# Five moves in a hand-written schedule: inputs, constants, values, slots and weight rows of a two-layer attention kernel

## The chip, the cores and the metric

The kernel runs on one core of a Trainium2 chip. The metric is the device time of one launch in microseconds (us). Three runs of the kernel before gave 1906.97, 1907.01 and 1912.09 us; the median is 1907.01.

## The reference

Sixteen batches of 256 tokens with 256 features (`x`) and a context of the same shape (`ctx`) pass through two layers, all in float32:

```python
x = x + xattn0(ctx, ln(x))     # 8 heads of 128; keys and values over [LN(ctx); LN(ln(x))], 512 rows
x = x + ffn0(ln(x))            # 1024 hidden, gelu; every batch has its own additions to W1 and W2:
                               #   products of rows 1..16 of ln(x), times a scale
x = x + xattn1(ln(x), ctx, ctx)   # one head of 256, softmax over 256 context rows
x = x + ffn1(ln(x))            # 8 experts of 256; sigmoid routing by zones, top 2 when no zone holds
```

The routing weights decide which expert serves which token. A token that an expert does not serve has weight zero there.

## The kernel before, in words

**Tiling.** A batch is two tiles of 128 tokens (TC = 2). Everything that must have features on the partitions is transposed in three steps: 32x32 blocks on VectorE (`to_blocks`, line 291), a write to DRAM (`hop`, line 296) and a read back in four DMAs (`from_blocks`, line 302). The probabilities of a head go the same way (`s2`, lines 863 and 867, and `s2_fetch`, line 876); the tile `tb` that holds their blocks has one buffer.

**The main loop** runs over 128 heads, n = 8b + h. One pass does: scores of head n (`s1`: sc, then maxima nm on VectorE, then exponentials on ScalarE), scaling by 1/sum on POOL (`s1_scale`), the fetch of head n-1's probabilities (`s2_fetch`), queries (`s0q`) and keys (`s0k`) of head n+1, the "bulk" of the head, the output product po of head n-2 (`s3`), and the transposes and hop of head n (`s2`). Evictions go through `evict`: to ScalarE, or to VectorE for a while after a gelu was emitted.

**Bulk.** In heads 2 to 5 a quarter of the values of heads 4-7 (pv), in heads 6 and 7 those of the next batch's heads 0-3, and in heads 0 to 4 one of the five steps of `inputs(b + 1)`: statistics of the context and its hop; statistics of x, normalised context and its hop; normalised x and its hop; and two steps of scaling on ScalarE into kvT.

**Chains and gaps.** What follows the eight heads of a batch is a generator `chain(b)`: output projection (px), layer norm (yb), the batch's own weights (W1e, W2e), hidden layer (ph), gelu, second product (pf), layer norm (yc), second attention (pv of WvT, pq of M1, scores, po), layer norm (row), routing logits (pl); then `route(b)`: weights, slot numbers (pn) and 16 indirect DMAs on POOL that write each token's row to its place in `slots_d`. Chains start at head 2 of the next batch and last nearly two batches, so that two chains and a route are open at once.

The planner keeps a count of TensorE time, `Clock.pe`, which each matmul raises. At each of six places of a head, `gap` runs units of the open jobs, oldest first, until 0.8 us of TensorE work were added. A unit ends with `yield w`: the job is not ready until `Clock.pe` has gone on by w. `SENT` (6.5) and `LANDED` (7.5) are the waits put behind a hop and behind its fetch. All of this fixes the program's order while it is built; on the chip each engine, and SP for the DMAs, takes its instructions in that order, and waits where data is missing.

**After the heads**, the same planner mixes the last chain with the experts (`experts`, class `G`): rows of one expert's slots are loaded (line 1082), transposed by a hop, multiplied (pg, pu, pd) and added to the output by indirect DMAs on POOL (line 1165). Groups of the second part of the batches (10 to 15) are loaded only after the route of batch 15 is done.

**The rows of the batch's own weights.** `chain` writes 8 rows of the layer norm to `ev_d` (lines 375 and 376) and reads them back to all 128 partitions as `ev` (line 380, 1 MB on the SBUF side). W1e (line 405, VectorE) and W2e (line 412, POOL; line 420, VectorE) are made of them and of `od` (line 397), which is taken from the transposed yb.

**The constants of the queries** are a product of yc with a row g1, summed (line 488): rc, used at the maxima of the second attention (lines 523 to 525).

Of the kernel before, what the change touches and what calls it, by code (L numbers as in the profile page):

```python
# [16 lines left out]
ALU = mybir.AluOpType  # L17
AX = mybir.AxisListType

P = 128  # L20
# [9 lines left out]
def xattn_ffn_kernel(  # L30
# [10 lines left out]
    nc = tc.nc  # L41
    B, S, D = x.shape
# [7 lines left out]
    TC = S // P  # L50
# [13 lines left out]
    wk = ctx.enter_context(tc.tile_pool(name="work_c", bufs=1))  # L64
# [49 lines left out]
    def gap(least=0.8, stand=0.0):  # L114
# [31 lines left out]
        out=before, in_=before, compare_op=ALU.is_gt, fill=0.0,  # L146
# [87 lines left out]
    g1 = keep.tile([P, D], F32, name="g1")  # L234
# [50 lines left out]
    def to_blocks(pool, src, C, tag, bufs, name, most=None):  # L285
        tb = pool.tile(
            [P, C * D], F32, tag=tag, bufs=bufs, name=name, padded_shape=[P, most or C * D]
        )
        tb = tb.rearrange("p (m d c s) -> p m d c s", m=QP, d=DC, c=C)
        for c in range(C):  # L290
            nc.vector.transpose(  # L291
                tb.rearrange("p m d c s -> p d m c s")[:, :, :, c, :],
                src[:, c, 0:D].rearrange("p (d m r) -> p d m r", d=DC, m=QP),
            )
        hop = dram.tile([P, QP, DC * C * QB], F32, tag=f"{tag}{C}", name=f"hop_{name}")
        nc.sync.dma_start(hop, tb.rearrange("p m d c s -> p m (d c s)"))
        return hop

    def from_blocks(dst, hop):
        from_ = hop.rearrange("(a r) m f -> m r a f", r=QB)  # L300
        for m in range(QP):
            nc.sync.dma_start(dst[ts(m, QB)].rearrange("r a d c s -> r a (d c s)"), from_[m])  # L302
# [22 lines left out]
    NA = D // NI  # L325


    behind_exp = []

    lasting = {}  # L330

    def chain(b, A, behind):
# [11 lines left out]
        def raw_tile(tag, name):  # L344
            return wk.tile([P, QP, DC, TC, QB], F32, tag=tag, name=name)
# [22 lines left out]
        while behind is not None and b - 1 not in A.fed:  # L368
# [2 lines left out]
        ln_apply(y, x_b, mv, rs)  # L371
        yp = wk.tile([32, NI, NA], F32, tag="yp", name=f"yp_{b}")
        nc.vector.tensor_copy(yp, y[0:32, 0, :].rearrange("p (a c) -> p c a", c=NI))
        ev_d = dram.tile([2 * NI, D], F32, tag="ev_d", name=f"ev_d_{b}")
        nc.sync.dma_start(ev_d[0:NI, :], y[1 : 2 * NI : 2, 0, :])
        nc.sync.dma_start(
            ev_d[NI : 2 * NI, :], yp[1 + 2 * NI : 4 * NI : 2, :, :].rearrange("p c a -> p (c a)")
        )
        ev = wk.tile([P, 2 * NI, D], F32, tag="ev", name=f"ev_{b}")
        nc.sync.dma_start(  # L380
            ev.rearrange("p n d -> p (n d)"),
            ev_d.rearrange("n d -> (n d)").partition_broadcast(P),
        )
        landed = Clock.pe + 15.0
        plus_row(x_b, lasting["b2"])
        hop = to_blocks(wk, y, TC, "tbc", 1, f"yb_{b}_b")
        yield SENT
        yTb = raw_tile("yT", f"ybT_{b}")
        from_blocks(yTb, hop)
        yT = in_order(yTb)  # L390
        yield landed - Clock.pe
        while behind is not None and b - 1 not in A.fed_forward:
            yield 0.4

# [89 lines left out]
        hop = to_blocks(wk, y, TC, "tbc", 1, f"yc_{b}_b")  # L484
        pr = wk.tile([P, TC, S], F32, tag="pr1", name=f"pr1_{b}")
        rc = small.tile([P, TC], F32, tag="rc", bufs=2, name=f"rc_{b}")
        for c in range(TC):
            nc.vector.tensor_tensor_reduce(
                out=pr[:, c, :], in0=y[:, c, :], in1=g1, op0=ALU.mult, op1=ALU.add,
                scale=1.0, scalar=g0, accum_out=rc[:, c : c + 1],  # L490
            )
        yield SENT
        yTc = raw_tile("raw_c", f"ycT_{b}")
        from_blocks(yTc, hop)
        landed = Clock.pe + LANDED


        v1 = wk.tile([P, TC, D], F32, tag="v1", name=f"v1_{b}")
        for m in range(TC):
            pv = mm_tile(D, f"pv1_{b}_{m}")  # L500
            for d in range(DC):
                mm(pv, cT[:, d, ts(m, P)], WvT[:, d, :], start=(d == 0), stop=(d == DC - 1))
            evict(v1[:, m, :], pv, None, None)
            yield
        yield landed - Clock.pe
        q1T = wk.tile([P, DC, S], F32, tag="q1T", name=f"q1T_{b}")
        for m in range(DC):
# [27 lines left out]
        pT = wk.tile([P, TC, S], F32, tag="pT1", bufs=1, name=f"pT1_{b}")  # L535
        for m in range(TC):
            evict(pT[:, m, :], in_order(raw)[:, m], None, None)
        yield 2.5
        mv = mv_tile("d")
        for c in range(TC):  # L540
            ri = small.tile([P, 1], F32, tag="ri1", name=f"ri1_{b}_{c}")
# [9 lines left out]

        rs = ln_rstd(mv, "d")
        nc.sync.dma_start(out[b].rearrange("(c p) d -> p c d", p=P), x_b)
        yield 2.8
        while b >= 2 and not A.tails[b - 2].done:
            yield 0.4
        row = A.row[b] = wk.tile([P, TC, ROW], F32, tag="row", bufs=2, name=f"row_{b}")
# [26 lines left out]
    def route(b, A, mine):  # L584
# [65 lines left out]
        serves, rest = tmp("serves"), tmp("rest")  # L650
        nc.vector.tensor_scalar(flat(serves), flat(wt), 0.0, None, ALU.is_gt)
        nc.vector.tensor_scalar(flat(rest), flat(wt), 0.0, None, ALU.is_le)
        yield 4.0

        pn = mm_tile(2 * TC * E, f"pn_{b}")
        mm(pn[:, 0 : TC * E], below, flat(serves), start=True, stop=True)
# [37 lines left out]
    with ExitStack() as sh, ExitStack() as sa, ExitStack() as sf:  # L694
# [315 lines left out]
        def bulk(b, h):  # L1010
            if h == 0:
                if b == 0:
                    filling["turns"] = all_turns()
                filling["in"] = inputs(b + 1) if b + 1 < B else None
            if h == 2:
                filling["v1"] = values(b, 1)
            if h == 6:
                filling["v0"] = values(b + 1, 0) if b + 1 < B else None
            if b == 0:
                load_late(h)  # L1020
                for _ in range(2):
                    advance(filling["turns"])
            if 2 <= h <= 5:
                advance(filling["v1"])
            if h <= 4:
                advance(filling["in"])
            if h == 7 and b + 2 < B:
                load_in(b + 2)
            if h >= 6:
                advance(filling["v0"])  # L1030
                yield
                advance(filling["v0"])
            yield
# [205 lines left out]
        for n in range(NS + 2):  # L1239
            b, h = divmod(n, H)  # L1240
            if h == 2 and b > 0:
                last = add_chain(b - 1, last)
            more = bulk(b, h) if n < NS else None
            if n < NS:
                s1(n)
            if n == NS - 4:
                sf.close()
                open_front()
                rest = Job(experts(
                    lists,  # L1250
                    lambda g: g.part == 0 or B - 1 in A.tails and A.tails[B - 1].done,
                ))
                line.append(rest)
            if n == NS - 1:
                sa.close()
                open_last_layer()
            while behind_exp:
                behind_exp.pop()()
            stand = 2.0 if n >= NS - 1 else 0.0
            gap(stand=stand)  # L1260
            if n < NS:
                s1_scale(n)
            if 1 <= n <= NS:
                s2_fetch(n - 1)
            if n + 1 < NS:
                s0q(n + 1)
            gap(stand=stand)
            if n + 1 < NS:
                s0k(n + 1)
            gap(stand=stand)  # L1270
            advance(more)
            gap(stand=stand)
            advance(more)
            gap(stand=stand)
            if n >= 2:
                s3(n - 2)
            gap(stand=stand)
            if n < NS:
                s2(n)
# [1 line left out]
        last = add_chain(B - 1, last)  # L1281
        line.append(rest)
        while line:
            while behind_exp:
                behind_exp.pop()()
            if D_.more is None and B - 1 in A.projected:
                sh.close()
                open_rest()
            gap(stand=1e9)
# [49 lines left out]
```

## Time and profile before

| what | value |
|---|---|
| median of three runs | 1907.01 us |
| profiled execution, its own time | 1906.59 us |
| its span | 1904.8 us |
| TensorE busy | 1824.0 us (96%) |
| VectorE busy | 1226.8 us (64%) |
| ScalarE busy | 593.1 us (31%) |
| POOL busy | 871.1 us (46%) |
| mean granted clock of TensorE | 0.989 |

The span runs from the first to the last instruction of the profiled execution. A row of the waits says: engine, what waited, its line, "<-", what ended the wait, and then us in total, times, longest. A row of the timeline says: start and duration in us, engine, line, operation, tile written <- tiles read, shapes, number of instructions merged, and in brackets the idle time before it with what ended it. Matmuls all stand on line 80 and are told apart by their tiles. A row of stretches gives the bounds, the length, busy time of PE, PEld, DVE, ACT and POOL with their counts, then the granted clock, the share of the DMA engines and GB/s. Heads of a batch begin with "sc<-kT,qT"; in batch 9, head 0 begins at 833.5, head 1 at 843.3, head 2 at 852.3, head 3 at 869.4, head 4 at 880.6, head 5 at 888.3 and head 6 at 898.8 us.

### The profile page before, as it was taken

What the parts mean: (1) busy time and instruction counts of PE and PEld (TensorE: products, weight loads), DVE (VectorE), ACT (ScalarE), POOL (GpSimd) and SP (SyncE); (2) the same over time, 40 slices, a digit from 0 to 9 for tenths busy, and PEclk for the clock granted to TensorE, in tenths of its full rate; (3) what the DMA queues carried; (4) which work ended last, traced back from release to release, by engine and by line L of the source; (5) the groups of instructions that cost most, each with busy time, mean ns of one, the idle gap of its engine ahead of it and who ended that gap; (6) DMA issues with size and microseconds to landing.
All of it is one profiled execution on the core that took longest, in us unless ns stands there. A gap on an engine that the chain in (4) does not pass through costs nothing. (4 is left out here: it accounts for less than half of the span.)

```text
span 1904.8 us, 22785 instructions
## 1 busy us (share of the span) xinstructions
PE 1824.0 (96%) x6568; PEld 1228.8 (65%) x6568; DVE 1226.8 (64%) x3324; ACT 593.1 (31%) x1323; POOL 871.1 (46%) x996
## 2 busy tenths in 40 slices
PE   8999999999999999999999999999999999899996
PEld 4666666666666666666666666666666767566665
DVE  4466586757575757585857575858574767565654
ACT  3433334333333333333333333333333212111110
POOL 2132226343535353535353535353534275767666
PEclk9999999999999999999999999999999999999999
DMA  6553536464636463636363636363636587999996
GB/s 214 177 188 122 167 133 216 140 200 136 200 131 204 133 213 130 199 126 212 128 216 128 212 127 203 126 214 126 219 118 202 157 224 194 232 246 234 216 206 109
DMA packets 274638, 336.92 MB, mean 177 GB/s; under 512 B 31772, under 2 KB 227272, under 8 KB 272456
## 3 DMA queue, kind: packets, MB, share of 16 engines
q1 hardware_dynamic: 243736, 283.82, 47.1%
q0 software_dynamic: 30720, 51.54, 11.4%
q8 instruction: 55, 0.90, 0.2%
q14 instruction: 79, 0.65, 0.1%
q10 hardware_dynamic: 48, 0.01, 0.0%
HBM read 167.87 MB, written 167.38 MB: 176 GB/s over the span
## 5 line engine op out<-in xcount | busy, mean ns | idle before, releaser
L855 POOL TENSOR_SCALAR pr<-pr,ri 128x512 f32<-128x512 f32 x256 | 182.5, 725 | 664.0 <-DVE ri L854 662.0
L847 ACT ACTIVATE pr<-sc,nm 128x512 f32<-128x512 f32 x256 | 173.5, 682 | 578.1 <-DVE nm L841 575.4
L674 POOL DMA_INDIRECT slots_d<-row,at_slot x256 | 255.6, 998 | 68.2 <-issue 68.2
L80 PE MATMUL sc<-kT,qT 128*128 128x512 f32 x512 | 253.1, 618 | 33.2 <-ACT kT L780 33.2
L80 PE MATMUL po<-pT,v 128*128 128x256 f32 x1024 | 243.3, 380 | 4.0 <-DMA pT<-hop 3.6
L1165 POOL DMA_INDIRECT out_dram<-o,at x128 | 200.0, 1563 | 99.2 <-DVE o L1164 27.1
L80 PE MATMUL pk<-kvT,Wk_sb 128*128 128x512 f32 x512 | 240.6, 592 | 0.0
L80 PE MATMUL pv<-Wv_sb,kvT 128*128 128x512 f32 x512 | 239.1, 596 | 0.1
L80 PEld LDWEIGHTS po<-pT,v 128*128 128x128 f32 x1024 | 194.4, 190 | 67.0 <-issue 37.7
L863 DVE STREAM_TRANSPOSE tb<-pr 128x512 f32<-128x512 f32 x256 | 165.6, 684 | 34.9 <-DMA hop<-tb 34.9
L80 PEld LDWEIGHTS sc<-kT,qT 128*128 128x128 f32 x512 | 98.0, 197 | 108.7 <-issue 64.8
L841 DVE TENSOR_REDUCE nm<-sc 128x1 f32<-128x512 f32 x256 | 160.3, 662 | 4.8 <-PE sc L80 3.8
L893 DVE TENSOR_SCALAR outT<-po,cvec 128x256 f32<-128x256 f32 x128 | 60.0, 469 | 157.8 <-PE po L80 137.6
L80 PEld LDWEIGHTS pv<-Wv_sb,kvT 128*128 128x128 f32 x512 | 95.6, 190 | 98.4 <-issue 89.0
L80 PEld LDWEIGHTS pk<-kvT,Wk_sb 128*128 128x128 f32 x512 | 97.3, 190 | 67.8 <-issue 61.2
L80 PE MATMUL pd<-wx,hTd 128*128 128x256 f32 x512 | 125.8, 383 | 9.9 <-DVE hTd L1151 7.9
L80 PE MATMUL pq<-kvT,Wq_sb 128*128 128x256 f32 x512 | 131.9, 380 | 0.0
L1140 ACT ACTIVATE sg<-pg 128x384 f32<-128x384 f32 (+3 forms) x82 | 41.2, 503 | 290.6 <-PE pg L80 242.8
L80 PE MATMUL pg<-yTd,wx 128*128 128x384 f32 (+3 forms) x328 | 125.1, 504 | 3.6 <-issue 3.0
L80 PEld LDWEIGHTS pq<-kvT,Wq_sb 128*128 128x128 f32 x512 | 97.5, 191 | 42.9 <-issue 31.3
L80 PEld LDWEIGHTS pd<-wx,hTd 128*128 128x128 f32 x512 | 97.4, 192 | 41.8 <-DVE hTd L1151 8.7
L80 PE MATMUL pu<-yTd,wx 128*128 128x384 f32 (+3 forms) x328 | 124.4, 502 | 0.0
(191 smaller groups left out, 2703.2 us busy)
## 6 DMA issues: line engine op xcount, KB each, us to landing
hop<-tb SPq DMA_DIRECT2D x128, 512.0 KB
pT<-hop SPq DMA_DIRECT2D x512, 128.0 KB
ev<-ev_d SPq DMA_DIRECT2D x16, 1024.0 KB
rows<-slots_d SPq DMA_DIRECT2D x31, 397.5 KB
hop_rows_b<-rows_b SPq DMA_DIRECT2D x30, 384.0 KB
yTd<-hop_rows_b SPq DMA_DIRECT2D x120, 96.0 KB
rows<-slots_d SPq DMA_DIRECT2D x8, 530.0 KB
cin<-in_ctx_dram SPq DMA_DIRECT2D x16, 256.0 KB
```

Of the source, the lines that this page charges most:

```text
L80: nc.tensor.matmul(out, lhsT, rhs, **kw)
L674: ins = nc.gpsimd.indirect_dma_start(out=slots_d[part], out_offset=bass.IndirectOffsetOnAxis(ap=at_slot[:, c, e : e + 1], axis=0), in_=row ...
L841: nc.vector.tensor_reduce(nm, sc, AX.X, ALU.max, negate=True)
L847: nc.scalar.activation(pr, sc, AF.Exp, bias=nm, accum_out=sm)
L855: nc.gpsimd.tensor_scalar(pr, pr, ri, 1.0, ALU.mult, ALU.mult)
L863: nc.vector.transpose(tb[:, :, c, :], heads[n][c][0].rearrange("p (m f) -> p m f", m=QP))
L893: nc.vector.tensor_scalar(o, po, col("bv", h), None, ALU.add)
L1140: nc.scalar.activation(self.sg, self.pg, AF.Tanh, scale=0.5)
L1165: ins = nc.gpsimd.indirect_dma_start(out=out_rows[0 : sum(NTOKS[: self.part + 1]), :], out_offset=bass.IndirectOffsetOnAxis(ap=self.at[:, ...
```

## The change

Five parts, and some waits of the planner with them:

1. *Inputs a step later*: the five steps of the next batch's inputs run in heads 1 to 5 instead of 0 to 4.
2. *Queries' constants behind their hop*: the two reductions of line 488 are emitted after the fetch of the transposed yc, and not before.
3. *Values of the second attention beside it*: its two value products and evictions are emitted right after the hop of yc is sent, and not after its fetch. The wait after the fetch is 9.0 instead of 7.5.
4. *Slots later*: `route` waits 12 instead of 4 before it numbers the slots, except for the last two batches.
5. *Weight rows behind a head's fetch*: yb's hop goes out ahead of the rows' writes to `ev_d`, and the read of `ev` is left to the main loop, which emits it behind the next head's `s2_fetch` (after the heads: at the next turn of the planner). The wait for it is counted from there, 12, and at least 7.5 after yb's own fetch.

Besides: 4.0 instead of 2.5 before the second attention's output product, and for the last batch 10.0 instead of 2.8 before the layer norm that goes into `row`.

```diff
@@ chain
         nc.vector.tensor_copy(yp, y[0:32, 0, :].rearrange("p (a c) -> p c a", c=NI))
+        hop = to_blocks(wk, y, TC, "tbc", 1, f"yb_{b}_b")
         ev_d = dram.tile([2 * NI, D], F32, tag="ev_d", name=f"ev_d_{b}")
...
-        nc.sync.dma_start(
-            ev.rearrange("p n d -> p (n d)"),
-            ev_d.rearrange("n d -> (n d)").partition_broadcast(P),
-        )
-        landed = Clock.pe + 15.0
+        landed = []
+
+        def rows_everywhere():
+            nc.sync.dma_start(
+                ev.rearrange("p n d -> p (n d)"),
+                ev_d.rearrange("n d -> (n d)").partition_broadcast(P),
+            )
+            landed.append(Clock.pe + 12.0)
+
+        behind_fetch.append(rows_everywhere)
         plus_row(x_b, lasting["b2"])
-        hop = to_blocks(wk, y, TC, "tbc", 1, f"yb_{b}_b")
         yield SENT
         yTb = raw_tile("yT", f"ybT_{b}")
         from_blocks(yTb, hop)
         yT = in_order(yTb)
-        yield landed - Clock.pe
+        while not landed:
+            yield 0.2
+        yield max(landed[0] - Clock.pe, LANDED)
...
-        for c in range(TC):
-            nc.vector.tensor_tensor_reduce(
-                out=pr[:, c, :], in0=y[:, c, :], in1=g1, op0=ALU.mult, op1=ALU.add,
-                scale=1.0, scalar=g0, accum_out=rc[:, c : c + 1],
-            )
-        yield SENT
-        yTc = raw_tile("raw_c", f"ycT_{b}")
-        from_blocks(yTc, hop)
-        landed = Clock.pe + LANDED
-
+        sent = Clock.pe + SENT
+        yield
 
         v1 = wk.tile([P, TC, D], F32, tag="v1", name=f"v1_{b}")
...
             yield
+        yield sent - Clock.pe
+        yTc = raw_tile("raw_c", f"ycT_{b}")
+        from_blocks(yTc, hop)
+        landed = Clock.pe + LANDED + 1.5
+        for c in range(TC):
+            nc.vector.tensor_tensor_reduce(
+                out=pr[:, c, :], in0=y[:, c, :], in1=g1, op0=ALU.mult, op1=ALU.add,
+                scale=1.0, scalar=g0, accum_out=rc[:, c : c + 1],
+            )
         yield landed - Clock.pe
...
-        yield 2.5
+        yield 4.0
         mv = mv_tile("d")
...
-        yield 2.8
+
+        yield 2.8 if b < B - 1 else 10.0
@@ route
-        yield 4.0
+        yield 12.0 if b < B - 2 else 4.0
@@ bulk
-            if h <= 4:
+            if 1 <= h <= 5:
                 advance(filling["in"])
@@ the main loop
                 s2_fetch(n - 1)
+            while behind_fetch:
+                behind_fetch.pop()()
             if n + 1 < NS:
                 s0q(n + 1)
...
-            while behind_exp:
-                behind_exp.pop()()
+            for late in (behind_exp, behind_fetch):
+                while late:
+                    late.pop()()
```

More of the change, by code (lines that the diff above doesn't have):

```diff
@@ L325, in xattn_ffn_kernel @@
     NA = D // NI
-    behind_exp = []
+    behind_exp, behind_fetch = [], []
     lasting = {}
```

## The prediction

> **What bounds the kernel now.** I read the page's busy shares first, then the waits of TensorE, then for the largest wait the order of time on each engine around one instance (batch 9), and last the clock rows.
>
> ```profile
> PE 1824.0 (96%) x6568; PEld 1228.8 (65%) x6568; DVE 1226.8 (64%) x3324; ACT 593.1 (31%) x1323; POOL 871.1 (46%) x996
> ```
>
> TensorE sets the time: 1824 of 1904.8 us. The change neither adds nor removes a matmul, so what can be won is TensorE's idle time, 81 us, and what slow clock adds to it. The waits view says whom it waits for (us in total, times, longest):
>
> ```profile
> PE sc L80 <- ACT kT L780: 33.2, 13, 2.8
> PE pd L80 <- DVE hTd L1151: 7.9, 2, 7.7
> PE pq L80 <- DMA ycT<-hop_yc_b: 4.4, 4, 1.7
> PE po L80 <- ACT pT L778: 3.1, 4, 1.2
> ```
>
> The first row is one wait a batch, from batch 4 on, always at the scores of head 2. VectorE's timeline of it in batch 9:
>
> ```profile
> 842.00 0.39 DVE L254 BATCH_NORM_STATS2 st_c<-cin 128x6 f32<-128x256 f32 x1
> 843.05 0.74 DVE L291 STREAM_TRANSPOSE cin<-cin 128x256 f32<-128x256 f32 x2
> ...
> 845.22 0.73 DVE L267 TENSOR_SCALAR yc<-x,mv_q,rs_q 128x256 f32<-128x256 f32 x2
> 845.86 0.76 DVE L291 STREAM_TRANSPOSE yc_b<-yc 128x256 f32<-128x256 f32 x2
> 846.55 1.02 DVE L488 CUSTOM_DVE_ANT_0 pr<-yc,g,g 128x256 f32<-128x256 f32 x1
> ...
> 847.91 1.29 DVE L863 STREAM_TRANSPOSE tb<-pr 128x512 f32<-128x512 f32 x2
> 849.13 1.25 DVE L841 TENSOR_REDUCE nm<-sc 128x1 f32<-128x512 f32 x2
> ```
>
> and the engine that waits for it:
>
> ```profile
> 852.32 1.98 PE L80 MATMUL sc<-kT,qT 128*128 128x512 f32 x4 [2.74 <-ACT kT L780]
> ```
>
> VectorE works without a gap from 842.0 to 850.4: first input step 1.8 us, slots 1.2 (844.08 to 845.30), yc and its transposes 1.5, constants of the queries (L488) 1.4, then tb and nm. Scores of head 1 are done at 845.2, their maxima start at 849.13. ScalarE's two exponentials wait for these, the q and k evictions (L780, to 852.26) stand behind them, and TensorE, which has 6.1 us of work in that head, stops.
>
> Measured as start of one matmul to start of the next, above that shape's usual distance, the twelve from 373 to 1424 us cost 33.7 us. Six are followed by 3.41 us of half clock, 1.7 us lost each, 10.2 in all:
>
> ```profile
> 755.30:758.70 3.40, 3.04 (x4) 1.50 (x5) 3.37 (x10) 0.30 (x1) 2.76 (x5) 0.50 0.60 191
> 852.20:855.60 3.40, 3.28 (x11) 2.17 (x12) 3.37 (x10) 0.06 (x1) 2.77 (x5) 1.00 0.66 210
> ```
>
> (the seventh figure is the granted clock: 0.50 after one such stop, 1.00 after the other). The Trainium skill, "TensorE: Matmul & The Clock Gate", HAM oscillation, warns of idle gaps over about 3.4 us. These stops are 2.4 to 2.9 us, so by the rule none drops the clock and the wait is worth 33.7; by the rows it is worth 43.9. I take the rows, for a new wait too.
>
> **The change, part by part.**
>
> *Relief before head 2.* Moved out of the stretch: input step 1.8, constants 1.4, slot arithmetic 1.2 = 4.4 us of VectorE, against a stop of 2.9. The two value groups (four matmuls, 0.86 us each) come in: TensorE gets 1.7 us more work there, ScalarE two evictions of 0.37 ahead of k. Slots need 12 instead of 4 us of TensorE work, which I follow to head 2. Batch 3 shows the same phase without the stop (queries normalised in head 1):
>
> ```profile
> 275.78 0.69 ACT L780 ACTIVATE kT<-pk,cvec 128x512 f32<-128x512 f32 x1
> ```
>
> k ends at 276.47, the scores start at 277.02 unhindered. With the values there k is 0.74 later and the scores 1.4 later (1.7 less the 0.28 of pn), margin about 1.2. Value: all of it, **-43.9**; if covered only half, -22.
>
> *Where the moved work lies.* Input steps issue the same VectorE work (1.8, then 2.6, then 2.0 us), hops of 0.4 and three fetches of four DMAs (1.8 to 2.9 us of SP each), a head later; the last, ScalarE's six copies (3.0 us), in head 5, still a head before the next batch's values. VectorE is busy 7.6 of head 3's 11.2 us and 3.6 of head 4's 7.7 (means of batches 5 to 12), so it fits: 0. POOL's 16 slot DMAs (1.0 us, 1.3 apart) slide from heads 2-4 to 2-5, where POOL is busy 1.9 of 10.1 us: 0; without that cover the W2 blocks (L412) behind them come 2.5 us late, in front of VectorE's w2_add. Constants are needed at the second attention's maxima, over 10 us later: 0.
>
> *Queries.* SP sends ycT at 857.61 in batch 9, behind an input fetch and a hop that now come a head later; in the new order it follows the first head's fetch and one hop, and TensorE asks at least 9 us of its work later (7.5 before). The waits at pq cost 6.5 us in seven batches; value **-6** (0 to -6.5).
>
> *The order that follows.* I traced the planner's clock by hand, with 1.71 us for scores, k and po, 0.85 for q. With the values gone from head 2 all four px units fit there, so yb is emitted in the first gap of head 3, 7 us of work earlier; heads 3 and 4 then hold only 7.7 us each. The wait of 4.0 moves po1 to the end of head 5 and, through row and hop, pl to the next head 0; the first FFN unit (ph) moves from head 6 to head 5.
>
> *Weight rows.* That is where I expect the loss. The 1 MB fetch ev is now issued after head 2's pT fetch, still in head 3, ahead of the second attention's hop, an input fetch and hop, and head 3's own hop; SP stands there until ev_d has landed, 1.5 us in batch 9 (879.87 to 881.40), and these stand behind it. SP and VectorE of batch 9 show what follows such a fetch:
>
> ```profile
> 881.40 0.35 SPq L380 DMA_DIRECT2D ev<-ev_d  x1
> 881.85 0.38 SPq L296 DMA_DIRECT2D hop_yb_b<-yb_b  x1
> 882.28 2.77 SPq L302 DMA_DIRECT2D pr1T<-hop_pr_b  x4
> 885.09 0.48 SPq L867 DMA_DIRECT2D hop<-tb  x1
> 892.46 1.73 SPq L876 DMA_DIRECT2D pT<-hop  x4
> ```
> ```profile
> 892.49 1.30 DVE L863 STREAM_TRANSPOSE tb<-pr 128x512 f32<-128x512 f32 x2 [3.47 <-DMA hop<-tb]
> ```
>
> The head's hop took 7.4 us and VectorE stood 3.5 us for its single buffer tb, 11 us after ev. Before, ph was a head away, so TensorE did not feel it. Counted from the start of head 5's scores in the new order: ev is issued 6.5 us ahead, with 0.25 MB more between it and the hop than here, so tb starts at +4.9, 11.4 after ev; tb 1.3, maxima 1.25, od 0.25, two W1e products 0.9 end at +8.6; TensorE has scores, q, k and v, 6.0 us, and then wants ph. It waits 2.6. The Trainium skill, "DMA: Bandwidth & Descriptors", Anatomy of one DMA, prices a DMA at 2.0 us plus bytes over 436 GB/s: 3.2 for the 512 KB hop, so landing 6.3 and not 11.4 us after ev's issue: no wait at all, and a time of 1844. The row has this very queue in it, so I lean to it: bounds 0 and 4, taken 2.4, and 0.5 a batch for half clock (fewer of these than of 2.9). 13 batches x 2.9 = **+37.7**. Behind od on VectorE stand ri (POOL's scaling waits for it) and the ph evictions; head 6 has 14.5 us and absorbs them. The po1 waits on ScalarE's pT (**-3.7**) go, as TensorE arrives later.
>
> *Last batch.* In the old order hop_yb_b stands behind ev and VectorE's pr_b waited for it at 1541.11, TensorE 3.1 us and 1.7 of half clock at 1542.9: hop first, **-4.8** (0 to -4.8). The row step:
>
> ```profile
> 1657.46 0.74 DVE L267 TENSOR_SCALAR row<-x,mv_d,rs_d 128x256 f32<-128x256 f32 x2 [11.86 <-POOL rs_d L262]
> ```
>
> rs_d is behind POOL's scatters (1.9 us apart), and everything on VectorE behind row. Ten instead of 2.8 us puts row 7.2 us of work later, within the time TensorE ran on (from 1645.6 to 1652): 7.9 and 2.3 of half clock go. But routing and slots of batch 15 come 7.2 later in the work, three more scatters (5.6 us) ahead of them, and SP already stood 6.5 us for them (rows issued at 1740.34) before the first groups of the second part. I give back 6 of 10.2: **-4** (+3 to -10).
>
> Sum: -43.9 - 6 - 3.7 - 4.8 - 4 + 37.7 = -24.7. The profiled execution took 1906.6 (span 1904.8 and 1.8 around it), the median is 1907.0: **1882**.
>
> **Rivals.**
>
> *B, rows hidden (0.26).* The hop lands as the page's price has it, or ev is gone before. What speaks for it: the engines move up to 420 GB/s around 890 us. Then about 0.7 a batch stays: -62.4 + 9 = 1853.
>
> *C, slower (0.16).* The same wait, one size larger: heads 3 and 4 are 15.4 us, in which some 5.6 MB must pass (ev 1.0, head hops and fetches 2.0, six quarter-MB transfers 1.5, slots 1.1) at 250 GB/s for ev and up to 420 for the rest. All gains are 62.4, over 13 batches 4.8 each: a wait of 3.1 with 1.7 of half clock after every one cancels them, and beyond 3.5 it is slower by over 0.3%. At 4.0: 13 x 5.7 = 74, 1918. Against it: the traced hop leaves 2.6, and only half of such stops met half clock.
>
> *D, the old wait stays in part (0.14).* 4.4 us are taken from a late stretch, but the value evictions precede k on ScalarE, and route's steps may fall in head 0's last gap. Half of it stays: 1882 + 22 = 1904; with a smaller row wait about 1895.
>
> **How the numbers follow.** A, the forecast, has 0.44 and its own range is 1866 to 1898. 0.3% of the time, 5.7 us, is about what a measurement can tell. Faster: A but 0.02, all of B, 0.08 of D: 0.76. Same: 0.02 of A, 0.05 of D, 0.02 of C: 0.09. Slower: 0.15. The range reaches into B, past its centre, and to the edge of C, leaving out about 0.08 below and 0.12 above: 1847 to 1912.
>
> **What would show it.** Right: no row of sc waiting for kT; pv of the second attention between q and the scores in heads 0 and 1; four px units in head 2, ph in head 5; a new TensorE wait at ph for W1e, behind od and tb; in the end no 11.9 us before row, but a longer stop of SP before the rows of part two. Wrong: the kT row still over 15 us, ph without a wait (then B), or ph waits over 3.5 us (then C).

## The result, and the profile after

The changed kernel takes 1918.37 us (median of 16 runs, 1905.23 to 1921.42), the kernel before beside it 1906.94 (16 runs): ratio 1.0046, 95% interval 1.0030 to 1.0062. It is slower by half a percent, where 1882 and a range of 1847 to 1912 were forecast. Its 16 runs lie in two groups, seven from 1905 to 1913 us and nine from 1918 to 1921, and the profiled execution (1918.5, span 1916.5 us, mean granted clock 0.978; 0.989 before) is of the upper one.

The page's busy shares, and the waits of TensorE (us in total, times, longest):

```profile
PE 1837.2 (96%) x6568; PEld 1242.2 (65%) x6568; DVE 1215.9 (63%) x3350; ACT 582.8 (30%) x1297; POOL 864.8 (45%) x996
```
```profile
PE ph L80 <- DVE W1e L412: 35.4, 13, 5.0
PE pg L80 <- DVE o L1173: 11.8, 2, 8.6
...
PE po L80 <- DMA pT<-hop: 4.0, 1, 4.0
PE pd L80 <- DVE hTd L1160: 2.0, 2, 1.8
```

The scores' wait for kT is gone, with those at pq and those at po for ScalarE's pT; one at po for a hop is left (4.0). The wait for hTd went from 7.9 to 2.0. In their place stand the two that the forecast named: the hidden layer (ph) waits for W1e, and the experts' products of the second part (pg) wait at the end. The 6568 matmuls are the same ones and keep TensorE busy 13 us longer: that is slow clock.

Batch 9 again, SP's queue, VectorE around the first ph, and that ph:

```profile
882.15 0.36 SPq L384 DMA_DIRECT2D ev<-ev_d  x1
882.61 0.38 SPq L296 DMA_DIRECT2D hop_pr_b<-pr_b  x1
883.04 2.45 SPq L302 DMA_DIRECT2D raw<-hop_cn  x4
885.59 0.50 SPq L296 DMA_DIRECT2D hop_xn<-xn  x1
886.19 0.77 SPq L876 DMA_DIRECT2D hop<-tb  x1
```
```profile
894.03 1.30 DVE L872 STREAM_TRANSPOSE tb<-pr 128x512 f32<-128x512 f32 x2 [4.44 <-issue]
895.26 1.25 DVE L850 TENSOR_REDUCE nm<-sc 128x1 f32<-128x512 f32 x2
896.44 0.21 DVE L404 TENSOR_SCALAR od<-ybT,scale_bc 128x16 f32<-128x16 f32 x1
896.68 1.24 DVE L412 SCALAR_TENSOR_TENSOR W1e<-ev,od,W1T 128x256 f32<-128x256 f32 x2
```
```profile
897.27 0.46 PE L80 MATMUL ph<-ybT,W1e 128*128 128x256 f32 x1 [2.19 <-DVE W1e L412]
```

Head 5 starts at 888.9, tb at +5.1 (forecast +4.9), ph at +8.4 (forecast +8.6): the traced chain is as it was worked out. The 4.44 us before tb are put down to "issue" here (no wait that the profile shows); the view of the tile `hop` says what tb waited for in all (us, times):

```profile
  DVE tb L872: 69.2, 15
```

What the stop cost is also in the clock. Stretches of 3.4 us around this stop (bounds, length, PE, PEld, DVE, ACT, POOL busy, granted clock, DMA share, GB/s):

```profile
895.30:898.70 3.40, 1.40 (x5) 0.97 (x6) 3.37 (x8) 2.39 (x6) 1.60 (x2) 1.00 0.83 231
898.80:902.20 3.40, 3.40 (x10) 2.69 (x9) 2.06 (x7) 1.98 (x5) 2.60 (x3) 0.50 0.75 260
```

A stop of 2.19 us, and then 3.4 us at half clock. There are 14 such stops at ph, one in head 5 of each batch from 2 to 15: the 13 of the row above and one of 1.7 us put down to "issue", 37 us together, 2.6 on average. At 12 of them the clock goes to half.

From the start of batch 3 to the start of batch 15 the kernel before takes 1147.7 us and the changed one 1147.4: 95.6 a batch in both. What the main loop won it lost, and all of the 11.7 us between the two profiles lies behind 1405 us.

### The profile page after: what moved, and what is told of

It reads as the page before. It is cut to its first block, busy times and chain, and to the rows that moved or that the text cites. A ratio compares the mean times of both kernels' runs of the same rounds, so it can differ in the third digit from the quotient of the medians.

```text
span 1916.5 us, 22738 instructions
## 1 busy us (share of the span) xinstructions
PE 1837.2 (96%) x6568; PEld 1242.2 (65%) x6568; DVE 1215.9 (63%) x3350; ACT 582.8 (30%) x1297; POOL 864.8 (45%) x996
## 5 line engine op out<-in xcount | busy, mean ns | idle before, releaser
L864 POOL TENSOR_SCALAR pr<-pr,ri 128x512 f32<-128x512 f32 x256 | 178.0, 706 | 436.1 <-DVE ri L863 432.8
L80 PE MATMUL po<-pT,v 128*128 128x256 f32 x1024 | 249.9, 388 | 4.0 <-DMA pT<-hop 4.0
L80 PEld LDWEIGHTS po<-pT,v 128*128 128x128 f32 x1024 | 201.3, 197 | 68.5 <-issue 33.2
L80 PE MATMUL sc<-kT,qT 128*128 128x512 f32 x512 | 240.9, 593 | 0.0
L872 DVE STREAM_TRANSPOSE tb<-pr 128x512 f32<-128x512 f32 x256 | 165.7, 685 | 69.2 <-DMA hop<-tb 49.4
L80 PE MATMUL ph<-ybT,W1e 128*128 128x256 f32 x512 | 140.0, 418 | 38.0 <-DVE W1e L412 35.4
L80 PEld LDWEIGHTS ph<-ybT,W1e 128*128 128x128 f32 x512 | 103.7, 207 | 88.0 <-issue 65.5
```

Source lines behind the costliest of these rows:

```text
L80: nc.tensor.matmul(out, lhsT, rhs, **kw)
L864: nc.gpsimd.tensor_scalar(pr, pr, ri, 1.0, ALU.mult, ALU.mult)
L872: nc.vector.transpose(tb[:, :, c, :], heads[n][c][0].rearrange("p (m f) -> p m f", m=QP))
```

## The experiments

Each was timed beside runs of the kernel before; ratios are to these. Fifteen kernels were run.

### Is it the read of the rows?

**The rows once.**

```diff
-        ev = wk.tile([P, 2 * NI, D], F32, tag="ev", name=f"ev_{b}")
+        if b == 0:
+            lasting["ev"] = wk.tile([P, 2 * NI, D], F32, tag="ev", name=f"ev_{b}")
+        ev = lasting["ev"]
...
-            nc.sync.dma_start(
-                ev.rearrange("p n d -> p (n d)"),
+            if b == 0:
+                nc.sync.dma_start(
+                    ev.rearrange("p n d -> p (n d)"),
```

> The changed kernel, but the 1 MB read of the weight rows (ev) is made for batch 0 only, and all later batches use batch 0's rows: 15 of 16 such reads are left out, and W1e and W2e are computed from the wrong rows, with the same instructions in the same order. T1 (the read, issued in head 3 ahead of that head's hop, makes the hop land late, VectorE stands for its single buffer tb, and od, W1e and the hidden layer behind it are late): the TensorE waits at ph for W1e (39.3 us over 14 batches in the changed kernel, about 62 with the half clock after them) fall below 8 us, VectorE's wait before tb in head 5 falls from 4.4 to below 1.5, and the time is 1850 to 1866. T2 (the hidden layer has been pulled into head 5, too close behind the transposed yb, wherever the rows come from): the waits at ph stay at 2 us or more each, and the time is 1905 to 1920.

Measured: 1852.2 us, ratio 0.9722 (0.9706 to 0.9739). One wait at ph is left, for another reason (5.4 us, for hT, at the end); VectorE's waits for the hop before tb fall from 69.2 us to 3.8, the clock is 0.992 and a batch takes 90.9 us. The two main loops as stretches, from the start of batch 3 to that of batch 15, the changed kernel first:

```profile
257.90:1405.30 1147.40, 1113.89 (x3985) 756.76 (x3984) 768.11 (x2137) 398.79 (x900) 497.14 (x636) 0.98 0.51 168
253.30:1344.20 1090.90, 1090.90 (x3985) 745.51 (x3984) 764.62 (x2137) 398.59 (x900) 494.96 (x636) 1.00 0.50 166
```

The same 3985 matmuls stand in the same order. Without the read TensorE never stops and has its full clock; with it TensorE is idle for 33.5 us and busy for 23.0 us longer. Over twelve batches that is 2.8 us of stops and 1.9 of slow clock in each. T1: the megabyte makes the waits. Without it the other changes win 4.7 us a batch, all that TensorE's stops and slow clock leave to win in this loop. What the kernel before takes without its read was not tried.

**The read behind the head's hop.**

```diff
         def rows_everywhere():
-            nc.sync.dma_start(
+            behind_hop.append(lambda: nc.sync.dma_start(
...
             if n < NS:
                 s2(n)
+            while behind_hop:
+                behind_hop.pop()()
```

> The changed kernel with one DMA moved: the read of the weight rows (ev) is issued at the end of head 3, behind that head's hop, and not ahead of it; every other instruction keeps its place, the bytes are the same. T1a (it is the place in the queue: the hop stands behind the megabyte): VectorE's wait for tb in head 5 (4.4 us) falls below 1, W1e is 2 to 4 us earlier, the waits at ph fall from 39 to below 15 us and the time is 1855 to 1885. T1b (it is the bytes: the DMA engines are full from 884 to 893 us, whatever comes first): the rows or ybT then land late themselves, the waits at ph stay over 30 us and the time is 1905 to 1920.

Measured: 1913.9 us, ratio 1.0023 (1.0009 to 1.0037). VectorE's timeline of batch 9 (head 5 starts at 881.8):

```profile
883.12 1.30 DVE L872 STREAM_TRANSPOSE tb<-pr 128x512 f32<-128x512 f32 x2 [0.68 <-DMA hop<-tb]
884.35 1.25 DVE L850 TENSOR_REDUCE nm<-sc 128x1 f32<-128x512 f32 x2
890.05 0.23 DVE L404 TENSOR_SCALAR od<-ybT,scale_bc 128x16 f32<-128x16 f32 x1 [4.45 <-DMA ybT<-hop_yb_b]
```

tb is in time, as T1a said. Now the transposed yb is behind the megabyte, od waits 4.45 us for it, and ph starts 9.1 us after its head did instead of 8.4. Inside this head the queue's order only picks who is late: T1b.

**Half of the read.** On the kernel with the last row's wait put back (below, 1907.6):

```diff
+            def half(i):
+                nc.sync.dma_start(
+                    ev[:, ts(i, NI)].rearrange("p n d -> p (n d)"),
+                    ev_d[ts(i, NI), :].rearrange("n d -> (n d)").partition_broadcast(P),
+                )
+
+            half(0)
+            behind_next.append(lambda: half(1))
```

> The run with the last row's wait put back, with one difference in the main loop: the read of the weight rows is cut in two. The half for W1e (512 KB on the SBUF side) is read where the whole was, the half for W2e behind the next head's fetch; TensorE's order is the same. T1b (the wait at ph is the time of the bytes ahead of the transposed yb and the hop on full DMA engines): half a megabyte less is 1.3 us at 380 GB/s up to 2.8 us at the half of the rate that the read itself had, so the waits at ph fall from 2.4 us a batch to 0 to 1.2, most half clocks behind them go, and the time falls by 25 to 55 us, to 1853 to 1883. Rival T10 (bytes are not what counts there; the wait comes from VectorE's own crowd in head 5): waits at ph over 1.8 us a batch stay, 1895 to 1912.

Measured: 1914.6 us, ratio 1.0018 (1.0007 to 1.0029). TensorE's waits:

```profile
PE po L80 <- ACT pT L791: 21.0, 13, 3.4
PE po L80 <- DMA pT<-hop: 13.5, 7, 5.7
...
PE ph L80 <- DVE W1e L416: 8.6, 5, 2.6
```

The waits at ph do shrink (all of them: 15.1 us in 12). But the second half is now in front of the fetch of the second attention's probabilities and beside a head's pT, and both output products wait for these. Both theories had the wrong time: the bytes count, and moving half of them moved the wait further down the same head (in batch 9 from 8.4 us after the start of head 5 to 11.7 and 14.8).

### Is it the hidden layer's place?

**A head and more later.**

```diff
-            landed.append(Clock.pe + 12.0)
+            landed.append(Clock.pe + 20.0)
```

> The changed kernel with a wait of 20 instead of 12 behind the read of the rows, so that the hidden layer begins in the first gap of head 7 instead of the last but one of head 5; the read stays ahead of head 3's hop. T1 (the read and its user are too close): the late hop is absorbed by VectorE's slack in heads 5 and 6, no wait at ph over 0.5 us, 1850 to 1870. T4 (the hidden layer meets VectorE's second attention and layer norm wherever it is put, as it did in head 6 of the run with the values put back): waits at ph of over 20 us in all, 1890 to 1915.

Measured: 1891.7 us, ratio 0.9893 (0.9868 to 0.9919). No wait at ph at all, as T1 said, but not T1's time; TensorE's largest row is now the second attention's output, which waits for its probabilities:

```profile
PE po L80 <- ACT pT L787: 17.8, 12, 3.0
```

ScalarE's timeline of batch 7 shows why:

```profile
699.89 1.09 ACT L757 ACTIVATE kvT<-raw,cvec 128x256 f32<-128x256 f32 x2 [6.07 <-DMA raw<-hop_xn]
700.88 0.69 ACT L780 COPY ctxT<-raw 128x256 f32<-128x256 f32 x2
701.48 0.71 ACT L787 COPY pT<-pr1T 128x256 f32<-128x256 f32 x2
```

ScalarE stands 6.07 us for the last input step (moved into head 5 by part 1), whose fetch is behind the read; pT is behind it. But the run does not try what was meant. The longer wait shifted the whole chain, and the read with it: in this batch it goes out at 689.50, in head 5 and behind the hop of head 3 (683.16), which it stood ahead of in the changed kernel. So the wait at ph may be gone by the layer's place or by the read's; this run does not tell them apart.

**Values put back.** The changed kernel with part 3 undone, so that the chain has its four values behind the fetch of yc again and ph comes in head 6:

```diff
-        sent = Clock.pe + SENT
-        yield
...
-        yield sent - Clock.pe
+        yield SENT
         yTc = raw_tile("raw_c", f"ycT_{b}")
         from_blocks(yTc, hop)
...
+        v1 = wk.tile([P, TC, D], F32, tag="v1", name=f"v1_{b}")
```

> The changed kernel with its third part undone: the two value products of the second attention come behind the fetch of the transposed yc again, so they fill head 2's gaps, the four px units spread into head 3, yb comes later and the hidden layer is back in head 6. The constants stay behind the fetch. T1: the wait at ph needs both the read and the pull into head 5, so with ph a head later it is below 0.5 us; the scores' wait for kT does not return, since inputs, slots and constants stay out of the stretch: 1850 to 1875. T3 (the values in head 2 were part of what made the wait for kT): it comes back with over 1.5 us a batch, 1880 to 1905.

Measured: 1915.0 us, ratio 1.0054 (1.0037 to 1.0071); neither theory. No kT wait came back, but ph waits in smaller pieces, 25.5 us in 20 for W1e and 10.7 in 12 for x: od starts 3.2 us after head 6 did, when its ybT has landed behind the read and an input fetch, and between the W1e products VectorE now has tb, nm and the second attention's output, which ended in the same head.

### Is it the read's place?

**The rows in their old place**, parts 1 to 4 kept:

```diff
-        hop = to_blocks(wk, y, TC, "tbc", 1, f"yb_{b}_b")
         ev_d = dram.tile([2 * NI, D], F32, tag="ev_d", name=f"ev_d_{b}")
...
+        nc.sync.dma_start(
+            ev.rearrange("p n d -> p (n d)"),
+            ev_d.rearrange("n d -> (n d)").partition_broadcast(P),
+        )
+        landed = Clock.pe + 15.0
         plus_row(x_b, lasting["b2"])
+        hop = to_blocks(wk, y, TC, "tbc", 1, f"yb_{b}_b")
```

> The changed kernel with its fifth part undone: rows written and read within the unit of yb, ahead of yb's hop, with the old wait of 15; parts 1 to 4 stay. T1: the read is then issued earlier, ahead of head 2's fetch of pT as well, with the same bytes still ahead of head 3's hop; VectorE's stand before tb shrinks by the earlier start, waits at ph of 1 to 2 us stay, and po of head 4 may wait for its pT up to 1.7 us a batch: 1895 to 1915. T2 (the place of the read alone makes the wait): no wait at ph over 0.5 us and 1850 to 1870.

Measured: 1917.6 us, ratio 1.0058 (1.0041 to 1.0074); dearer than T1 had it, and not T2. ph does not wait, but the scores do, 32.0 us for kT, and po 20.1 us for pT. It is another kT wait, in head 5: yb's hop is behind the read, its blocks and those of the second attention's probabilities (pr_b) share one buffer, and VectorE stands 7.48 us for that hop, with the maxima, the exponentials and kT behind.

**Part 5 alone**, on the kernel before:

```diff
+        hop = to_blocks(wk, y, TC, "tbc", 1, f"yb_{b}_b")
         ev_d = dram.tile([2 * NI, D], F32, tag="ev_d", name=f"ev_d_{b}")
...
-        nc.sync.dma_start(
-            ev.rearrange("p n d -> p (n d)"),
...
+        behind_fetch.append(rows_everywhere)
         plus_row(x_b, lasting["b2"])
-        hop = to_blocks(wk, y, TC, "tbc", 1, f"yb_{b}_b")
...
-        yield landed - Clock.pe
+        while not landed:
+            yield 0.2
+        yield max(landed[0] - Clock.pe, LANDED)
...
+            while behind_fetch:
+                behind_fetch.pop()()
```

> The kernel before with part 5 alone (the rows' read behind a head's fetch, yb's hop ahead of their writes). The order of the units stays as before, so the scores of head 2 go on waiting for kT (33 us), and the hidden layer stays in head 6, behind 7 us more TensorE work. T1: no wait at ph, and only the small gains of the fifth part: po1 for pT and the last batch's 4.8 us: 1897 to 1908. T2 (the fifth part costs wherever it is put): waits at ph or po1 of 1 us or more in each batch, 1915 to 1925.

Measured: **1856.6 us, ratio 0.9740 (0.9724 to 0.9757)**. Both theories are off by 40 us or more. The longer wait for the rows puts ph 4.7 us later in head 6, the whole chain follows, and yc now comes behind the maxima that head 2's scores wait for (batch 9):

```profile
824.88 1.30 DVE L870 STREAM_TRANSPOSE tb<-pr 128x512 f32<-128x512 f32 x2
826.10 1.25 DVE L848 TENSOR_REDUCE nm<-sc 128x1 f32<-128x512 f32 x2
827.28 0.72 DVE L267 TENSOR_SCALAR yc<-x,mv_q,rs_q 128x256 f32<-128x256 f32 x2
827.91 0.77 DVE L291 STREAM_TRANSPOSE yc_b<-yc 128x256 f32<-128x256 f32 x2
828.59 1.03 DVE L495 CUSTOM_DVE_ANT_0 pr<-yc,g,g 128x256 f32<-128x256 f32 x1
```

The kT row is down to 3.0 us, none of it in head 2, and a batch takes 91.6 us. Is this the shift, or the place of the read? Two more kernels have TensorE's order of this run from batch 2 to batch 14.

**The shift alone.**

```diff
-        landed = Clock.pe + 15.0
+        landed = Clock.pe + 18.0
```

> The kernel before with nothing but a wait of 18 instead of 15 ahead of od and W1e. From batch 1 to batch 14 TensorE's instructions then stand in exactly the order of the run with part 5 alone, but the rows are read in their old place. T7 (part 5 alone won its 50 us by the shift of the chain, which takes yc and the slots out of the crowd ahead of head 2's scores, not by the place of the read): no wait at kT, 1855 to 1868. T9 (the read's place won it): the wait at kT or one at po for pT stays at over 1.5 us a batch, 1880 to 1905.

**The shift, and yb's hop ahead of the rows**, whose read follows at once:

```diff
+        hop = to_blocks(wk, y, TC, "tbc", 1, f"yb_{b}_b")
         ev_d = dram.tile([2 * NI, D], F32, tag="ev_d", name=f"ev_d_{b}")
...
-        landed = Clock.pe + 15.0
+        landed = Clock.pe + 18.0
         plus_row(x_b, lasting["b2"])
-        hop = to_blocks(wk, y, TC, "tbc", 1, f"yb_{b}_b")
```

> The run with the wait of 18 and one line moved: yb's blocks and their hop go out ahead of the rows' writes and of their read, which follow at once, in the same unit (not behind the next head's fetch). TensorE's order is that of the run with the wait of 18, which took 1965.7. T9a (what cost there was the hop that frees the block buffer, queued behind the read): VectorE's wait of 10.8 us before pr_b falls to 1 to 3, the wait at kT in head 5 is below 0.5, and the time is 1855 to 1866, that of part 5 alone. T9b (the read must also be behind the next head's fetch): the 2 hops and the fetch behind the read are late instead, kT or pT waits of 1 us or more a batch stay, 1870 to 1900.

Measured: 1965.7 us, ratio 1.0305 (1.0288 to 1.0323), and 1917.7 us, ratio 1.0029 (1.0018 to 1.0039), both slower than either of their theories had it. Batch 9 of the shift alone, VectorE and then TensorE:

```profile
912.38 0.77 DVE L291 STREAM_TRANSPOSE pr_b<-pr 128x256 f32<-128x256 f32 x2 [10.77 <-DMA hop_yb_b<-yb_b]
```
```profile
917.45 1.22 PE L80 MATMUL sc<-kT,qT 128*128 128x512 f32 x1 [8.62 <-ACT kT L780]
```

The same line of VectorE with part 5 alone:

```profile
853.07 0.77 DVE L291 STREAM_TRANSPOSE pr_b<-pr 128x256 f32<-128x256 f32 x2 [1.24 <-DMA hop_yb_b<-yb_b]
```

And with the hop first, SP's queue in batch 9, and TensorE's largest row:

```profile
882.74 0.35 SPq L381 DMA_DIRECT2D ev<-ev_d  x1
883.19 0.37 SPq L296 DMA_DIRECT2D hop_pr_b<-pr_b  x1
883.92 0.32 SPq L867 DMA_DIRECT2D hop<-tb  x1
892.34 0.80 SPq L876 DMA_DIRECT2D pT<-hop  x2
```
```profile
PE po L80 <- DMA pT<-hop: 41.5, 14, 6.5
```

One order of TensorE and three places of the read: 1965.7, 1917.7 and 1856.6 us. In all three head 2 has lost its stop. With the read ahead of yb's hop, the block buffer is late, and the scores of head 5 wait. With the read right behind that hop, head 3's own hop is late, and SP cannot issue its fetch before 892.34 (T9b in kind). Behind the next head's fetch, what stands behind the read has a head to spare. T9 was right that the place counts, but not with the kT wait of before: the shift takes away the old stop, the place avoids a new one.

### What was the relief worth?

Three kernels with TensorE's order of before: part 1 alone, part 2 alone, and both.

```diff
-            if h <= 4:
+            if 1 <= h <= 5:
                 advance(filling["in"])
```
```diff
-        for c in range(TC):
-            nc.vector.tensor_tensor_reduce(
...
         landed = Clock.pe + LANDED
+        for c in range(TC):
+            nc.vector.tensor_tensor_reduce(
```

> The kernel before with part 1 alone (the next batch's inputs a step later); TensorE's order of instructions is unchanged. As the forecast reckons, 1.8 us of VectorE's work leave the stretch ahead of head 2's scores, so the stop at kT (2.7 us a batch, 33 in all) shrinks to about 0.9, 12 in all, and the half clock behind it goes: 20 to 31 us less, 1876 to 1887. Rival T8 (the stop is moved on, since the steps' hops and fetches now meet the rows' read in heads 4 and 5): new waits of as much, 1895 to 1910.

> The kernel before with part 2 alone (the two reductions for the queries' constants behind the fetch of the transposed yc, ahead of the values); TensorE's order is unchanged. 1.4 us leave the stretch: the stop at kT shrinks to about 1.3, 17 in all, the half clock goes: 16 to 27 us less, 1880 to 1891. If VectorE takes them up in another place that is as tight, no change: 1902 to 1910.

> The kernel before with parts 1 and 2; TensorE's order is unchanged. 3.2 us leave the stretch, more than the stop of 2.7: no wait at kT, no half clock, and the waits at pq smaller: 1858 to 1868. T8 as above: 1880 to 1905.

Measured: part 1 alone 1908.8 us, ratio 1.0013 (1.0003 to 1.0023), kT row 26.9 us; part 2 alone 1879.9, ratio 0.9850 (0.9833 to 0.9867), kT row 16.2; both 1886.0, ratio 0.9892 (0.9875 to 0.9909), kT row 10.1. So part 1 is worth nothing by itself (T8's time) and costs 6 to 8 us on top of part 2, though the kT row falls each time. The constants are worth what was worked out. The input step is not: with it gone, VectorE's next line in batch 9 is

```profile
843.02 0.48 DVE L893 TENSOR_SCALAR outT<-po,cvec 128x256 f32<-128x256 f32 x1 [1.05 <-PE po L80]
```

an eviction that has to wait for TensorE. It started at 843.72 before, 0.4 us after its head did, and now 0.2 us before: of 1.8 us only 0.55 arrive at the maxima. And the steps hinder elsewhere: with both parts pv waits 6.6 us for hT and po 8.9 us for pT (3.1 before).

**Parts 5 and 2**, by the same two edits together:

> The kernel before with parts 5 and 2; TensorE's order is that of part 5 alone. Part 2 alone won 26 us where TensorE waited for kT in head 2. With part 5 alone that wait is already gone from the main loop (90.9 us a batch against 90.9 with no read at all), so by the reading that the parts pay only for the same stop, nothing is left to win: 1852 to 1861. If the parts add up: 1828 to 1838.

Measured: 1863.2 us, ratio 0.9736 (0.9718 to 0.9754), the ratio of part 5 alone. On average a batch takes 91.6 us in both profiles (the 90.9 above holds for single batches of part 5 alone). The parts pay for one stop, once.

### The last batch

**2.8 again, in the changed kernel**, and **10.0 on part 5 alone**:

```diff
-        yield 2.8 if b < B - 1 else 10.0
+        yield 2.8
```

(and the reverse in the second).

> The changed kernel with 2.8 instead of 10.0 ahead of the last batch's layer norm; the main loop is untouched. T5 (the 10.0 lost more than it won: SP's stand for the slots of batch 15 grew from 6.5 to 15 us and TensorE's wait at the second part's first products from 0.7 to 8.7 us, with 10 us of half clock behind it): a wait of 8 us for row comes back, SP's stand and the 8.7 shrink below 8 and 2, and the time falls by 4 to 10 us, to 1908 to 1914. Rival T6 (the tail is longer because the whole last chain ends later in the new order, whatever this wait): 1915 to 1922.

> The kernel before with part 5 and the 10.0 ahead of the last batch's layer norm, nothing else. By the forecast's bookkeeping the wait for hTd (9.8 us with part 5 alone) falls below 3 and SP's stand before the rows of the second part grows by 6 us, which TensorE feels: 1849 to 1856, 3 us below part 5 alone. Rival: all of it comes back at the second part's first products, 1856 to 1866.

Measured: 1907.6 us, ratio 0.9999 (0.9987 to 1.0011), so 10.8 us less than with the 10.0 (9.0 by the ratios); and 1866.1, ratio 0.9775 (0.9760 to 0.9790), 9.5 more than without it (6.7 by the ratios). The first is T5's case; the second is the rival's, at its edge. Without the 10.0 the whole change is worth nothing, either way. SP's longest stand in the tail, in the changed kernel and with 2.8:

```profile
SPq L1091 <- DMA slots_d<-row,at_slot: 15.0, 1, 15.0
```
```profile
SPq L1091 <- DMA slots_d<-row,at_slot: 6.0, 1, 6.0
```

With 2.8 TensorE stops 9.7 us for row, at 1654.7; with 10.0 it stops 8.57 us at the second part's first products, at 1757.2, and its clock there is at half for 10 us. The wait did not vanish, it moved behind SP's stand. The stretches from the start of batch 15 to the end, before, changed, and changed with 2.8:

```profile
1405.30:1904.80 499.50, 467.22 (x1711) 321.54 (x1710) 301.01 (x845) 87.64 (x189) 300.23 (x245) 0.97 0.79 199
1405.30:1916.50 511.20, 473.39 (x1727) 324.82 (x1726) 300.35 (x853) 88.46 (x192) 299.69 (x245) 0.96 0.78 195
1391.60:1899.30 507.70, 472.57 (x1727) 325.76 (x1725) 300.09 (x853) 88.36 (x192) 299.68 (x245) 0.96 0.77 196
```

So by these profiles, one execution each, the 10.0 costs 3.5 us of the tail (7.0 with part 5 alone, 508.9 to 515.9), and 8.2 of the 11.7 are there without it: T6 has a share. The changed kernel without the read has a tail of 505.6 us, so some 5.6 are the read's: head 5 of batch 15, with stops of 2.1 and 4.0 us and 10 us of half clock, lasts 21.0 us with it and 16.4 without. The rest is open. Nor is all of the 10.8 in the tail: the profiled execution with 2.8 (1901.1, below its median) took 94.6 us a batch in the main loop, though TensorE's order there is that of the changed kernel.

## Why the prediction was wrong

The order came nearly as traced: four px in head 2, ph in head 5, pl in the next head 0, 7.7 us for heads 3 and 4; only the values stand both in head 1, and not in heads 0 and 1. The sum was -24.7 us and the two profiles differ by +11.7. Of these 36 us, 16 lie between the starts of batches 3 and 15 (forecast -15.9, measured -0.3) and 20 behind (forecast -8.8, measured +11.7).

- **Weight rows (+37.7): this step failed, in one term.** The wait was right in kind and nearly in size: 2.6 was worked out, 2.4 taken, 2.8 a batch measured in the main loop. The 0.5 a batch for half clock was wrong: it is 1.9. I argued that shorter stops would meet half clock less often than the six of twelve before; 12 of 14 did. Together 4.7 a batch and not 2.9, 56 us over twelve batches. The rule that I set against the trace (the Trainium skill, "TensorE: Matmul & The Clock Gate", HAM oscillation: idle gaps over about 3.4 us) would have put the loss lower still. The trace was the better guide, but I read it for the stop's length, and the length alone does not decide (last section). The price taken from the Trainium skill, "DMA: Bandwidth & Descriptors", Anatomy of one DMA, 3.2 us for the hop, was far off; nor is it this hop's, since that section's fit is for DMAs that GpSimd issues, and SP issues this one. It went out at 886.19, and VectorE, which waits for its buffer, could go on at 894.03; in these 7.8 us the DMA engines were 98% busy.
- **The last batch (-4.8 and -4): wrong in sign.** The tail behind batch 15's start went from 499.5 to 511.2 us. "I give back 6 of 10.2" failed: more came back than was won, 3.5 to 7.0 us by the tails of the profiles. Left out was the half clock behind the moved stop (10 us at half). The -4.8 did not arrive either: at 1546.8 TensorE stops as before, now 2.7 us for an expert's weights. And the wait at ph was counted for the main loop, but head 5 of batch 15 has it too.
- **Relief before head 2 (-43.9), queries (-6), po1 (-3.7): right in sum, not in the working.** The rows are gone, and without the read twelve batches take 56.8 us less than before; 53.6 were reckoned over thirteen. But of the 4.4 us moved off VectorE only 2.4 arrive at the maxima of head 1 in batch 9:

```profile
850.58 1.25 DVE L850 TENSOR_REDUCE nm<-sc 128x1 f32<-128x512 f32 x2
```

This is 3.5 us after the head's start, and 5.8 before. Other steps of `route` stand there now, and the input step had stood ahead of an eviction that waits for TensorE anyway. What made it enough is that yc comes behind these maxima and that TensorE, with the values in this head, asks for the next scores 1.5 us later. kT is ready 0.6 us ahead of them; the margin was put at 1.2. (The 7.6 and 3.6 us of VectorE in heads 3 and 4 add up instructions that overlap; it is busy for 7.0 and 3.3.)

That C's number, 1918, came out is luck. C got there with stops of 4.0 and half clock after each, 5.7 a batch, and with the last batch's gain; measured are 4.7 a batch, which cancel the gains of the main loop, and a last batch that lost. B's 1853 is near what the kernel takes without the read (1852.2), by other terms as well: that run has no waits at ph in the loop and a longer tail.

## What to carry to other kernels

When stops are removed by moving work, list what each transfer is queued behind in the new order, and give a large read a stretch in which all that stands behind it has a head to spare: with one and the same order of TensorE in the main loop, its place was worth some 108 us. Before adding the durations in front of a late instruction, look for the wait among them; what stands ahead of a wait is worth only the part by which it outlasts that wait. Try each part by itself: one of the five, alone, was 2.6% faster than before, and all five were slower.

## What the runs showed of the hardware

**The half clock goes by windows.** In every trace the half clock begins on a grid of 3.41 us (each trace has its own start). Laid over TensorE's idle time between matmuls, in the main loops (257 to 1405 us) of the kernel before, the changed one and the fifteen runs:

```
TensorE idle in a window    windows    next window at half clock
under 1.5 us                   5589        5
1.5 to 2.0                       32        8
2.0 and more                     78       78
```

The five of the first row are themselves at half clock and go on so. So a stop counts by how much of it falls into one window; between 1.5 and 2.0 us these runs do not say what decides. Of the stop shown above 1.94 us lie in one window, and 0.50 follows. One of 2.13 us in batch 5 of the same kernel, ending at 514.5, lies across two and leaves the clock alone:

```profile
509.70:513.10 3.40, 2.69 (x7) 0.90 (x5) 1.82 (x4) 0.08 (x1) 1.93 (x2) 1.00 0.66 208
513.10:516.50 3.40, 1.95 (x8) 1.44 (x9) 3.37 (x10) 2.39 (x6) 1.61 (x3) 1.00 0.83 245
516.50:519.90 3.40, 3.40 (x18) 2.99 (x17) 3.06 (x7) 2.44 (x6) 2.93 (x4) 1.00 0.72 259
```

**Eight kernels take 28 windows a batch.** 28 x 3.413 is 95.6 us. The kernels before, after, with the rows in the old place, with the values back, with the read behind the hop, with part 1 alone, with half the read and with the hop first took 95.58 to 95.86 us a batch, though their stops are at different places and of different sizes; in the last of them the half clock came back every 95.6 us:

```profile
320.80:324.20 3.40, 3.40 (x9) 2.35 (x8) 0.48 (x1) 0.20 (x2) 0.00 (x0) 0.50 0.50 168
416.40:419.80 3.40, 3.40 (x9) 2.69 (x9) 0.07 (x1) 0.96 (x3) 0.00 (x0) 0.50 0.67 238
512.00:515.40 3.40, 3.40 (x9) 2.69 (x10) 0.00 (x0) 0.86 (x3) 0.00 (x0) 0.51 0.69 244
```

That a loop with a stop of some 2 to 3 us settles on the grid, because the loss depends on where in the window the stop lies, is argued from this and was not tried. Three of the runs speak against it as the whole story: with the values back only one window of the loop is at half clock, with half the read three, and they take 95.6 and 95.8 as well; and the changed kernel with 2.8, with stops of 2.4 us at ph, took 94.6. If it holds, small gains inside such a loop show nothing until the stop is short enough, as with part 2 alone (93.9 us a batch, stops of 1.25 us and no half clock in the loop).
